# Normed queries and keys turned by VectorE's block transpose, through DRAM

## The chip, the cores and the metric

The kernel runs on one core of one Trainium2 chip. The core has TensorE (PE, matrix products), VectorE (DVE), ScalarE (ACT), GpSimd (POOL) and SyncE (SP, which here only issues transfers), and 16 DMA engines that move data between DRAM and the on-chip memory. The metric is the time of one execution on the device in microseconds, as the median of several runs.

## The reference, cut to what matters

`x` is 64 batches of 32 tokens with 512 channels, all in fp32. Four layers are added to it one after the other; the change concerns the third, attention with a paged cache of keys and values:

```python
q = rmsnorm(x @ Wq.T) * q_norm_w      # 32 heads of 128
k = rmsnorm(x @ Wk.T) * k_norm_w      # 8 heads of 128
v = x @ Wv.T
pos = cache_seqlens[:, None] + arange(32)
q, k = rope(q, pos), rope(k, pos)     # rotary: halves of 64 swapped and mixed
k_all = concat([k_cache[block_table], k])     # 16 pages of 32, then 32 new keys
v_all = concat([v_cache[block_table], v])
scores = (q @ k_all.T) / sqrt(128)    # 4 query heads share one key head
probs = softmax(where(valid, scores, -1e30))
x = x + (probs @ v_all) @ Wo.T
```

The other layers are a product with one of 16 small matrices per batch before it and after it, and a linear layer with low-rank additions.

## The kernel before, in words

**Tiling.** Four batches make a tile of 128 tokens, so there are 16 tiles. The eight key heads are cut into two groups of four. A *step* is one group and one tile (32 steps: all tiles of the first group, then all of the second); a *unit* is one batch of a step (128 units, of four key heads each). Two steps with neighbouring tiles make a *pair* (16 pairs).

**Order.** The whole order is written by hand. The program is a list of *slots*; `at(slot, place, what)` files a piece of work, and `slot(i)` emits the pieces of slot `i` in a fixed order of places on in-order engines. From slot 0 on, slot `i` computes the scores of one key head of one unit (two products, L839 and L842, 128 query rows by 544 keys), evacuates them with the mask (VectorE, L847), and takes the exponentials (ScalarE, L858). `flip` turns the shares of two slots ago on TensorE (L881, copied by VectorE at L883), and the values of three slots ago are multiplied (L891). Four slots are a unit, 16 a step, 32 a pair. In the same slots TensorE also projects the queries, keys and values of the next pair (L655): three blocks of seven products, one block for keys and values, two for two query heads each, put together by a two-level scheme that needs fewer products, whose sums VectorE makes (`take`, L667). Slots below 0 are the front: the first two layers for all tiles, turning the key pages of the first group, and the first pair's projections. After the last slot the output products (L1342) run alone.

**Norm and rotary before.** A tile of four heads (128 tokens, 4 x 128) goes through `Norm`: squares on ScalarE (L711), the power -1/2 on GpSimd (L716, L718), then on VectorE `scale` (L723), `straight` (L730), `swapped` (two halves, L742) and `sum` (L752). There are 160 such tiles: per pair two of keys and eight of queries. `norm_piece` is a small planner: called three times a slot, it takes the next piece if the slot's count of VectorE work (`busy`) allows. One slot after `sum`, `turn` makes four 128x128 transposes on TensorE (L757) into PSUM, and `keep` copies them with ScalarE (L769) into a tile that stays on chip: `qT_0`, `qT_1` for queries, `kT_new` for new keys. `begin` copies a batch's new keys into the 17th page of the unit's keys (L826).

**Transfers.** SyncE issues most transfers, in program order. `Unit` takes a keys' tile `kT` (two buffers) and issues 16 page loads of 64 KB, each with a page number read from a table (L787, L795). It does so four slots before the unit's first scores. Also on SyncE: `fetch_new` (a batch's new values, L817), the values' stores (L697), rotary tables (L595), the activations (L590), for the second group's pages a load and two transfers per page tile during the first group (L255, L288, L292), and the outputs of half the heads (L931). GpSimd issues the value gathers (L105) and the other outputs, and makes the masks (L810).

## Time and profile before

| | |
|---|---|
| three runs | 2455.72, 2458.07, 2463.95 us, median 2458.07 |
| profiled execution, first to last instruction (the one time recorded of it) | 2459.1 us, granted TensorE clock 0.999 |
| first scores (slot 0) | at 190 us |
| one pair of steps, middle of the run | 118 us |
| output products alone, about 2080 to the end | 379 us |
| DMA | 459 MB in 457888 packets, 187 GB/s on average |

The profile names an engine, a source line, the operation and the tiles it writes and reads (out<-in), with a count and durations. "SPq" rows are SyncE issuing transfers; the time is that of the issue, not of the transfer. A timeline row with xN merges N instructions, and its duration runs from the first one's start to the last one's end.

### The profile page before, as it was taken

The numbers are of one execution on the slowest core, as the hardware profiler recorded it, in microseconds if no ns is written. First come the engines' busy times: TensorE is split into PE (matmuls) and PEld (weight loads), VectorE is DVE, ScalarE is ACT, GpSimd is POOL, SyncE is SP. The second block draws the span as 40 slices with busy tenths as digits, with TensorE's granted clock in tenths as the row PEclk, the third lists the DMA queues.
The fourth block names the chain that finished last, engine by engine and source line by source line (L and its number), as shares of the span: only waits on it lengthen the run. The fifth ranks groups of instructions, "written<-read, shape, count | busy, mean of one in ns | idle before, by whom it ended". The sixth has DMA issues, their size and how long they took to land.

```text
span 2459.1 us, 47105 instructions
## 1 busy us (share of the span) xinstructions
PE 2414.3 (98%) x13760; PEld 1863.4 (76%) x13760; DVE 1671.4 (68%) x3604; ACT 1399.1 (57%) x4005; POOL 1188.6 (48%) x1163
## 2 busy tenths in 40 slices
PE   7998999999999999999999999999999999999999
PEld 4556777777777777777777777777777788888887
DVE  5766777777867777787777777777777766333222
ACT  2236767677777777677777777777676764000000
POOL 4435556555555556655556555556565663000000
PEclk9999999999999999999999999999999999999999
DMA  7876666666667677866666666566667874233221
GB/s 258 273 233 195 187 199 192 202 193 192 199 188 208 189 214 221 262 184 198 175 192 176 189 179 192 170 193 175 190 179 233 256 248 155 104 112 129 86 88 59
DMA packets 457888, 459.18 MB, mean 187 GB/s; under 512 B 52960, under 2 KB 381024, under 8 KB 453920
## 3 DMA queue, kind: packets, MB, share of 16 engines
q1 hardware_dynamic: 402560, 276.03, 37.0%
q0 software_dynamic: 55072, 180.14, 24.1%
q8 instruction: 111, 1.82, 0.3%
q14 instruction: 145, 1.19, 0.2%
HBM read 384.66 MB, written 79.69 MB: 189 GB/s over the span
## 4 chain that ended last, share of the span: by engine, by line
PE 90%; DMA 3%; issue 2%; DVE 2%; ACT 2%; SPq 1%; POOL 1%; DVEq 0%; ACTq 0%; POOLq 0%
PE proj_ps L655 22%; PE o_ps L891 17%; PE out_ps L1342 15%; PE s_ps L839 9%; PE pT_ps L881 8%; PE s_ps L842 8%; PE l_ps L494 3%; PE head_ps L757 3%; PE o_ps L904 1%; DMA kT<-kT 1%; DMA o<-oT 1%; SPq L795 1%; PE s_ps L874 1%; PE h_ps L478 1%; PE mix_ps L438 1%
## 5 line engine op out<-in xcount | busy, mean ns | idle before, releaser
L105 POOL DMA_INDIRECT v_sb<-v,v_rows x512 | 545.1, 1065 | 369.0 <-PE o_ps L891 255.0
L891 PE MATMUL o_ps<-pT,v_sb 128*128 128x128 f32 x4096 | 625.5, 275 | 7.9 <-DMA v_sb<-v,v_rows 3.2
L891 PEld LDWEIGHTS o_ps<-pT,v_sb 128*128 128x128 f32 x4096 | 576.8, 191 | 39.7 <-ACT oT L923 6.4
L858 ACT ACTIVATE sm<-sm,top 128x544 f32<-128x544 f32 x512 | 380.8, 744 | 320.7 <-DVE top L847 242.6
L847 DVE CUSTOM_DVE_ANT_0 sm<-s_ps,pen 128x544 f32<-128x544 f32 x512 | 369.0, 721 | 113.1 <-PE s_ps L842 98.8
L864 ACT ACTIVATE sm<-sm,share 128x512 f32<-128x512 f32 x512 | 369.9, 722 | 109.5 <-DVE share L863 73.9
L883 DVE COPY pT<-pT_ps 128x512 f32<-128x512 f32 x512 | 352.9, 689 | 69.3 <-PE pT_ps L881 22.9
L839 PE MATMUL s_ps<-kT,qT 128*128 128x288 f32 x1024 | 334.9, 409 | 2.4 <-DMA kT<-kT 1.3
L881 PE MATMUL pT_ps<-ident,sm 128*128 128x128 f32 x2048 | 309.7, 274 | 5.5 <-ACT qT L769 4.0
L842 PE MATMUL s_ps<-kT,qT 128*128 128x256 f32 x1024 | 304.9, 379 | 1.7 <-DMA kT<-kT 1.4
L667 DVE TENSOR_TENSOR raw<-proj_ps,raw 128x512 f32<-128x512 f32 x332 | 224.1, 687 | 114.5 <-PE proj_ps L655 103.2
L839 PEld LDWEIGHTS s_ps<-kT,qT 128*128 128x128 f32 x1024 | 179.2, 191 | 149.8 <-issue 129.1
L810 POOL TENSOR_SCALAR pen<-key_f,seq_f 128x544 f32<-128x544 f32 x128 | 283.7, 2216 | 12.8 <-DMA kT<-kT 1.5
L881 PEld LDWEIGHTS pT_ps<-ident,sm 128*128 128x128 f32 x2048 | 238.7, 141 | 9.6 <-ACT qT L769 5.2
L711 ACT ACTIVATE sq<-raw 128x128 f32<-128x128 f32 x640 | 198.5, 310 | 74.5 <-DVE raw L667 58.8
L842 PEld LDWEIGHTS s_ps<-kT,qT 128*128 128x128 f32 x1024 | 194.6, 190 | 56.4 <-issue 2.3
L863 DVE RECIPROCAL share<-total 128x1 f32<-128x1 f32 x512 | 83.6, 163 | 177.4 <-ACT sm L858 149.7
L716 POOL TENSOR_SCALAR ss<-ss 128x4 f32<-128x4 f32 x160 | 40.2, 251 | 326.3 <-ACT sq L711 320.0
L1392 ACT COPY p<-out_ps 128x256 f32<-128x256 f32 x7 | 2.6, 372 | 333.5 <-PE out_ps L1342 333.5
L655 PE MATMUL proj_ps<-sum,x 128*128 128x512 f32 x380 | 189.1, 600 | 0.0
L105 POOL DMA_INDIRECT mix_rows<-in_w,cond_rows x32 | 34.8, 1087 | 307.6 <-DVE mix_diag L170 299.5
L718 POOL TENSOR_TENSOR rstd<-ss,minus_half 128x4 f32<-128x4 f32 x160 | 167.8, 1049 | 13.3
(177 smaller groups left out, 3571.1 us busy)
## 6 DMA issues: line engine op xcount, KB each, us to landing
kT<-kT SPq DMA_DIRECT2D x2048, 64.0 KB
o_in<-o SPq DMA_DIRECT2D x28, 1024.0 KB
o<-oT POOLq DMA_DIRECT2D x69, 256.0 KB
o<-oT SPq DMA_DIRECT2D x58, 256.0 KB
page_rows<-in_kv_cache SPq DMA_DIRECT2D x32, 256.0 KB
v<-in_kv_cache SPq DMA_DIRECT2D x32, 256.0 KB
kT<-page_rows SPq DMA_DIRECT2D x32, 256.0 KB
vn<-raw SPq DMA_DIRECT2D x32, 256.0 KB
```

Of the source, the lines that this page charges most:

```text
L105: nc.gpsimd.indirect_dma_start(out=dst, out_offset=None, in_=table, in_offset=bass.IndirectOffsetOnAxis(ap=index, axis=0),)
L655: nc.tensor.matmul(self.ps, lhsT=self.pair.x[x][:, c if x == "b" else half.start + c, :], rhs=blocks(self.b)[w][:, c, :], start=(c == 0), ...
L810: nc.gpsimd.tensor_scalar(self.pen, key_f, seq_f[:, self.b : self.b + 1], BIG, ALU.is_ge, ALU.mult)
L839: nc.tensor.matmul(ps[:, first:HID], lhsT=q, rhs=self.kT[:, :n1, k, :], start=True, stop=True)
L842: nc.tensor.matmul(ps[:, HID : first + LA], lhsT=q, rhs=self.kT[:, n1:, k, :], start=True, stop=True)
L847: nc.vector.tensor_tensor_reduce(out=sm, in0=ps[:, first : first + LA], in1=self.pen, scale=1.0, scalar=3e38, op0=ALU.add, op1=ALU.min, ac ...
L858: nc.scalar.activation(sm, sm, AF.Exp, bias=top, scale=-1.0, accum_out=total)
L864: nc.scalar.activation(sm[:, :L], sm[:, :L], AF.Copy, scale=share)
L881: nc.tensor.transpose(ps[:, c, :], self.sm[k][:, c * P : (c + 1) * P], ident)
L883: nc.vector.tensor_copy(pT, ps)
L891: nc.tensor.matmul(o_of[self.s, k][:, self.j, :], lhsT=self.v[c][:, k * D : (k + 1) * D], rhs=self.pT[k][:, c, :], start=(self.j == 0 and ...
L1342: nc.tensor.matmul(ps[:, :HALF], lhsT=o[:, i, :], rhs=w[i // REP][:, i % REP, :], start=(i == 0), stop=(i == KG * REP - 1),)
```

## The change

The four-head tiles are normed in pairs, as tiles of 128 x (2 x 4 x 128): for queries, the two four-head tiles of one step that belong to one block; for keys, the tiles of the two steps of the pair. So there are 80 `Norm`s in place of 160, with 128x1024 operations. `sum` is moved from VectorE to GpSimd. `turn` becomes one VectorE transpose of 32x32 blocks: since a batch has 32 tokens, a block's rows are one batch, and the transposed block is 32 of the 128 head channels for that batch. `store` then writes it to a DRAM tile `qk`, four transfers for a tile of queries (one a batch) and eight for keys (one a batch and step), all on SyncE. The transfer puts the four blocks of 32 channels under one another. `fetch_heads` loads a batch's new keys and queries (128 x 640) behind the pages of its keys' tile, two slots before its first scores, and `scores` reads both from there. The tiles `kT_new`, `qT_0`, `qT_1`, the four TensorE transposes per tile, their evacuation and the copy in `begin` are gone. The planner gets costs per piece and takes any piece that is ready; projections start six slots ahead of a pair's window instead of one (`AHEAD`), and the front begins five slots earlier. The order between slots is otherwise as it was.

```diff
+    qk_dram = [
+        [dram.tile([NB, D, (1 + KG) * P], F32, name=f"qk_{g}_{t}") for t in range(NT)]
+        for g in range(NG)
+    ]
...
             def new(self):
-                return proj_pool.tile([P, REP, D], F32, name="raw", bufs=6)
+                return proj_pool.tile([P, 2, REP, D], F32, name="raw", bufs=4)
...
             def sum(self):
-                nc.vector.tensor_tensor(self.a, self.a, self.b, ALU.add)
+                a, b = [x.rearrange("p i h d -> p (i h d)") for x in (self.a, self.b)]
+                nc.gpsimd.tensor_tensor(a, a, b, ALU.add)
 
             def turn(self):
-                self.tp = ps_t.tile([P, REP, P], F32, name="head_ps", tag="t")
-                for h in range(REP):
-                    nc.tensor.transpose(self.tp[:, h, :], self.a[:, h, :], ident)
...
+                self.turned = self.raw.rearrange("p i h d -> p (i h d)").rearrange(
+                    "p (c m s) -> p c m s", c=NC, s=S
+                )
+                nc.vector.transpose(
+                    self.turned, self.a.rearrange("p i h (c e) -> p c (i h) e", c=NC)
+                )
+
+            def store(self):
+                pair = self.block.pair
+                for i in (0, 1) if self.i == KV else (self.i,):
+                    step = pair.steps[i]
+                    if self.i == KV:
+                        heads, first, n = slice(i * REP, (i + 1) * REP), 0, P
+                    else:
+                        heads, first, n = slice(0, 2 * REP), (1 + 2 * self.block.b) * P, 2 * P
+                    for j in range(NB):
+                        nc.sync.dma_start(
+                            out=qk_dram[step.g][step.t][j][:, first : first + n].rearrange(
+                                "(c e) f -> e c f", c=NC
+                            ),
+                            in_=self.turned[j * S : (j + 1) * S, :, heads, :].rearrange(
+                                "e c m s -> e c (m s)"
+                            ),
+                        )
...
-                self.kT = room["kT"].tile([P, NPP + 1, KG, PSIZE], F32, name="kT")
+                self.kT = room["kT"].tile([P, NPP + 1 + KG, KG, PSIZE], F32, name="kT")
...
+            def fetch_heads(self):
+
+                nc.sync.dma_start(
+                    out=self.kT[:, NPP:].rearrange("p n k s -> p (n k s)"),
+                    in_=qk_dram[self.g][self.t][self.j],
+                )
...
-                q = step_of[self.s].qT[k][:, self.j].rearrange("p h s -> p (h s)")
+                q = self.kT[:, NPP + 1 + k].rearrange("p h s -> p (h s)")
...
+        ROOM = 2.0
+        COST = {"scale": 1.2, "straight": 1.2, "swapped": 1.3, "turn": 1.2}
+        NEXT = {"scale": "straight", "straight": "swapped", "swapped": "turn"}
 
         def norm_piece(slot):
 
 
-            if not pieces or pieces[0][0] > slot or busy.get(slot, 0) >= 2 + (slot % 4 == 1):
+            for piece in pieces:
+                ready, norm, name = piece
+                if ready <= slot and busy.get(slot, 0) + COST[name] <= ROOM:
+                    break
+            else:
                 return
-            busy[slot] = busy.get(slot, 0) + 1
...
+            busy[slot] = busy.get(slot, 0) + COST[name]
+            getattr(norm, name)()
+            at_piece = pieces.index(piece)
+            if name == "turn":
+                pieces.pop(at_piece)
+                at(slot, "store", norm.store)
+                return
+            later = name == "swapped"
+            if later:
+                at(slot + 1, "take", norm.sum)
+            pieces[at_piece] = (slot + 2 * later, norm, NEXT[name])
...
-        AHEAD = 1
+        AHEAD = 6
...
         n = KG * len(units)
-        begin = -WINDOW - AHEAD - 10
-        ready = -6
+        front = -WINDOW - AHEAD
+        begin = front - 10
+        ready = front + 27
...
+            at(KG * u - 2, "fetch", call, unit_of, u, "fetch_heads")
             at(KG * u - 2, "act", call, unit_of, u, "begin")
```

## The prediction

> **What bounds the kernel now.** I read the page's first part, then the busy time by stage, then single queues. TensorE first:
>
> ```profile
> PE 2414.3 (98%) x13760; PEld 1863.4 (76%) x13760; DVE 1671.4 (68%) x3604; ACT 1399.1 (57%) x4005; POOL 1188.6 (48%) x1163
> ```
>
> A busy PE need not be PE at its peak, so the stages decide (PE, PEld, DVE, ACT, POOL busy; clock; DMA share; GB/s). The two long ones are one pair of steps each, 32 slots:
>
> ```profile
> 554.00:672.00 118.00, 117.73 (x717) 90.45 (x716) 89.20 (x199) 85.41 (x249) 66.56 (x64) 1.00 0.66 196
> 1498.00:1616.00 118.00, 117.76 (x715) 90.33 (x715) 89.59 (x200) 85.06 (x248) 66.87 (x64) 1.00 0.62 184
> 1970.00:2010.00 40.00, 38.25 (x273) 33.83 (x272) 23.33 (x55) 25.44 (x61) 26.11 (x27) 1.00 0.87 270
> ```
>
> In a pair TensorE idles 0.3 us of 118 at full clock: what is taken from it there is time, until another queue comes due. The transposes stand in the timeline of TensorE:
>
> ```profile
> 566.06 1.02 PE L655 MATMUL proj_ps<-sum,x 128*128 128x512 f32 x2
> 566.92 0.60 PE L757 MATMUL head_ps<-ident,rot_a 128*128 128x128 f32 x4
> 567.36 0.65 PE L839 MATMUL s_ps<-kT,qT 128*128 128x288 f32 x2
> ```
>
> Start to start, four cost 0.44 us, 0.11 each (the 273 ns of one is pipeline depth). They aren't hidden: the next scores start behind them.
>
> The engine that no busy share counts is SyncE, which only issues. Its timeline in the first group:
>
> ```profile
> 705.16 0.57 SPq L817 DMA_DIRECT2D v_new<-vn  x1
> 705.79 0.60 SPq L288 DMA_DIRECT2D v<-in_kv_cache  x1
> 706.49 0.55 SPq L292 DMA_DIRECT2D kT<-page_rows  x1
> 707.91 10.03 SPq L795 DMA_DIRECT2D kT<-kT  x16
> 717.99 0.61 SPq L817 DMA_DIRECT2D v_new<-vn  x1
> 722.71 9.41 SPq L795 DMA_DIRECT2D kT<-kT  x16
> 732.17 0.42 SPq L255 DMA_DIRECT2D page_rows<-in_kv_cache  x1
> 737.29 0.87 SPq L931 DMA_DIRECT2D o<-oT  x2
> 738.25 0.57 SPq L817 DMA_DIRECT2D v_new<-vn  x1
> 740.36 9.80 SPq L795 DMA_DIRECT2D kT<-kT  x16
> ```
>
> A unit's 16 key loads hold the queue 10.0 us out of 14.75 (four slots). Over 672 to 790 the eight loads' rows sum to 78.9 us, the other rows to 14.0, gaps of 0.06 between rows and some 0.8 of page-number reads before each unit add 8.3: 101.2 us of 118. In 1500 to 1617, where no pages are turned any more, the same count gives 97.0 of 117. SyncE is 83 to 86% full, and in order. Today that rarely shows:
>
> ```profile
> PE s_ps L842 <- DMA kT<-kT: 1.4, 2, 1.2
> PE s_ps L839 <- DMA kT<-kT: 1.3, 1, 1.3
> ```
>
> (waits of TensorE: total us, times, longest). In 1970 to 2010, where slots are short, TensorE already falls to 96% as key loads follow each other without a pause.
>
> **The change, part by part.**
>
> *Transposes.* 640 x 0.11 = -70 us of TensorE: 4.4 a pair, 66 in the fifteen full pairs, 4 in the front. Nothing replaces them on TensorE. A pair could fall from 118.1 to 113.7 in the first group and from 117.2 to 112.8 in the second: 14.2 and 14.1 a unit, 3.55 a slot.
>
> *ScalarE.* 160 evacuations (L769, 91.4 us) and 128 key copies (L826, 37.5 us) go: off the path, worth nothing in time.
>
> *VectorE.* Per tile, one scale 0.706, one straight 0.690, two halves of swapped 0.432 and one sum 0.749 make 3.0 us, 482 in all. Per double tile: a 128x1024 product took 1.21 (L619), so 1.21 + 1.21 + 2 x 0.69 = 3.8 us, 304 for 80, plus the block transposes, which the trace lacks. The nearest row is again the 128x1024 pass at 1.21: 97 us. The Trainium skill, "VectorE: DVE Perf Modes", section "The three transpose paths", speaks against that: 311 ns for one 128x128, which times eight is an estimated 2.5 us, 199 in all. By the row VectorE falls from 89.3 to 84.3 us a pair, by the rule it rises to 90.6; both stay under 113.7, so either gives zero. I take the row.
>
> *GpSimd.* The sum doubles L450's 128x512 (1.28 undisturbed): 2.5 us x 80 = 200, against 80 fewer power pairs (1.05 + 0.25): -104. GpSimd goes from 67 to 73 us a pair. But its two-input pass stops VectorE's: beside an L450 of 1.35 us (127.91 to 129.26) the L723 product that started at 128.05 took 1.76 instead of 0.67. By the planner's costs (ROOM, COST) two sums of the five in a pair stand in the same slot as the next tile's scale. Behind it on VectorE wait the takes and the next evacuation of scores, which TensorE needs one slot later. VectorE has 30 us of room a pair, so I take 0; the bound is rival two.
>
> *SyncE, the step that decides.* New per pair: 24 stores (8 for the keys, 4 for each of 4 query tiles) and 8 head loads. The stores lay 32 partitions into four row groups in DRAM, like L292 (0.55, the same kind of split); with the gap 0.61. Bounds: 0.39 (the plain o<-oT, 0.33) to 0.66 (L288, 0.60). A head load is a plain row load: 0.38 (L590), with gap and one more semaphore 0.45. Sum: 24 x 0.61 + 8 x 0.45 = 18.2 us, so 119.4 in the first group and 115.2 in the second: more than TensorE needs. The Trainium skill, "DMA: Bandwidth & Descriptors", section "Issuing engines are not separate DMA queues", calls the sequencer's time to initiate a DMA "usually small relative to the DMA itself". By that rule these steps cost nothing and the total would be about 2400; here the issue (0.35 for a key load) is longer than its 128 packets take on 16 engines (about 0.036 each by the queue's totals, 0.3), so I go by the row.
>
> Room is not shared freely: the keys' tile has two buffers, so a unit's loads can't start before the scores two units back end, and must land before its own begin, 16.65 us later (five slots less 1.1 of scores). Issue 10.05 and landing 1.3 (packet records) leave 5.3 us for lateness and everything between, as the head load stands behind. With the planner's slots (from a pair's first score):
>
> - Slots 0-3: last pair's 4 query stores, head load, rotary, values, o: the next window starts 4.8 late, and 4-7 leave 8-11 2.5 late.
> - Slots 8-11, the keys' eight stores: 2.5 + 10.05 + 4.9 + v_new 0.63 + 0.45 + 1.3 = 19.8, so TensorE waits 3.2.
> - Slots 20-23: 2.8 + 10.05 + 0.4 + 2.45 + 0.45 + 1.3 = 17.45: 0.8.
> - Slots 28-31: 3.4 + 10.05 + 0.43 + 2.45 + 0.63 + 0.45 + 1.3 = 18.7: 2.0.
> - The others fit. First group: 5.9 a pair. Second group, without page transfers (3.5 us): 3.1 + 1.0 = 4.1.
>
> The wait of the first store in a burst for VectorE's turn is met, as SyncE reaches it behind 10 us of loads. The head load in slot 30 needs stores issued in slot 28; the one it reads went first of four and has some 3 us to land: zero, at most 1.5 a pair. What is late next: a raw buffer is free only when its stores have landed; the copy in slot 5 needs the one stored at slot 0, with about 3 us left. Beyond that ScalarE, and the exponentials behind its copy, would stand.
>
> *DMA.* 42 MB written and 42 read again, at the hardware queue's 276 MB for 37%: 11% of the span, so about 0.66 becomes 0.8. Below the 0.87 of the tail: zero.
>
> *Order moved (AHEAD).* All of the front and every projection move five slots ahead. In the tail five slots lose their filler, where SyncE needs 13 us a unit anyway, and the last pair's stores and heads (2.45 + 8 x 0.45) join it: +7. At 180 to 210 TensorE now works 21 of 30 us before the first scores; the moved projections fill some of that, while sum, store, landing and head load (2.5 + 2 + 1.5, estimates from the rows above) lengthen the first tile's way: +4, so the front gives its 4 back.
>
> **Sum:** -70 + 8 x 5.9 + 7 x 4.1 + 7 + 4 = +17, on the profiled execution's span of 2459.1, which lies 1 above the runs' median of 2458.1: **2476**.
>
> **Rivals.**
>
> 1. *Not slower: issuing is cheaper.* At 0.50 a store the same windows give -18, at 0.40 about -46, thus 2412; 0.55 is the break-even. For it: plain rows cost 0.33 to 0.38, the query stores read one contiguous 4 KB row per partition. Against: every four-way DRAM split of SyncE in the trace cost 0.55 to 0.58 (L292, L817).
> 2. *VectorE becomes the bound.* If all five sums hold VectorE for 2.5 us where 1.5 of slack exists, 5 us a pair, 75 in all. Alone, with SyncE free, -70 + 11 + 75 = +16; on top of SyncE, half of it hidden behind its waits, 2510 to 2550. For: the 1.76. Against: by then the sum is mostly done when scale starts.
> 3. *It balances:* stores at 0.55, within 0.3% (7.4 us, about what a measurement can tell).
>
> That the change takes nothing off the path is excluded by the 0.3 us of idle.
>
> **How the numbers follow.** Forecast 0.50 (own range 2455 to 2515; 0.05 of it within 0.3%), cheaper issue 0.28 (2405 to 2450), VectorE or ScalarE on top 0.15 (2515 to 2570), balance 0.07. Faster 0.28, same 0.12, slower 0.60. Leaving out the outer part of both ends: 2415 to 2545.
>
> **What the next profile would show.** Right: no head_ps; DVE transposes near 1.2; TensorE waits for kT of several us a pair, once behind eight stores in slots 8-11; SyncE without pauses; store issues near 0.55. Wrong: TensorE still at 99% in a pair of about 114 (stores under 0.5), or waits on top or oT (VectorE, ScalarE) ahead of kT.

## The result, and the profile after

The changed kernel takes **2864.98 us** (median of four runs, 2861.84 to 2866.92) against 2456.89 us for the kernel before on the same chip (2453.82 to 2463.95). The ratio is **1.1654** (95% interval 1.1635 to 1.1673), so it is 17% slower. The prediction had the sign and missed the size: 2476, range 2415 to 2545. Its profiled execution spans 2865.1 us.

The first part of the page after, as shown of before:

```profile
PE 2487.0 (87%) x13120; PEld 1879.1 (66%) x13120; DVE 1648.9 (58%) x3204; ACT 1308.3 (46%) x3717; POOL 1347.9 (47%) x1083
```

No engine became the bound. TensorE issues 640 instructions fewer, yet its busy time rose by 73 us, and it now idles 378 us of the span (45 before). The busy time by stage says why both are so (one pair of steps of the first group, one of the second, and the stretch of the last group that was shown of before; columns as there):

```profile
491.00:637.00 146.00, 124.62 (x676) 92.36 (x676) 86.81 (x174) 79.76 (x229) 76.13 (x59) 0.92 0.66 194
1351.00:1493.00 142.00, 118.65 (x653) 88.69 (x652) 85.19 (x170) 76.91 (x222) 77.84 (x59) 0.92 0.63 187
1970.00:2010.00 40.00, 33.88 (x176) 25.28 (x175) 25.13 (x49) 21.82 (x66) 20.79 (x16) 0.96 0.54 153
```

A pair takes 142 to 146 us in place of 118. TensorE stands for 21 to 23 us of it, and the granted clock is 0.92 and no longer 1.00: what it does, it does more slowly. What TensorE waits for (total us, times, longest):

```profile
PE s_ps L905 <- DVE top L878: 93.2, 31, 6.2
PE s_ps L870 <- DMA kT<-qk: 71.0, 16, 13.3
PE s_ps L870 <- DMA kT<-kT: 62.5, 15, 11.5
PE s_ps L870 <- issue: 47.6, 13, 7.2
```

L870 is the first product of the scores, which needs a batch's pages and heads; L905 is the transpose of the shares of the new keys. The prediction knew of the first place only. SyncE's waits and ScalarE's, the same columns:

```profile
SPq L823 <- PE s_ps L873: 134.3, 39, 7.7
SPq L705 <- DVE raw L675: 105.7, 17, 11.7
...
SPq L793 <- DVE raw L780: 31.7, 22, 11.9
```

```profile
ACT oT L954 <- DMA o<-oT: 116.1, 23, 7.2
```

SyncE stands 106 us in front of the values' store (L705), until VectorE has made the last sum of that tile, and 32 us in front of stores of turned tiles (L793). ScalarE's wait for an output tile's buffer was 3.1 us in three times before; it is 116 now. The two places in the kernel before:

```profile
ACT oT L923 <- DMA o<-oT: 3.1, 3, 1.6
```

```profile
SPq L697 <- DVE raw L667: 2.1, 2, 1.8
```

**Where the 406 us between the two spans went.** TensorE's idle time between the first and the last scores rose from 19 to 338 us: +216 ahead of scores, +111 ahead of L905, -9 elsewhere. The first scores start at 211.8 us and not at 190.5: +21. The transposes give about 3.4 us a pair back (worked out below): -52 in fifteen and a half pairs. What follows the start of the last scores is the same (394.5 before, 394.0 after). The remainder, 406 - 318 - 21 + 52 = **119 us**, is what matrix products lost to the clock: 287 us of the attention ran at half clock, 3 before. A count that doesn't use the remainder agrees: TensorE is busy for 235 of these 287 us, and half of that is 117.

**The two waits in the timeline.** First a late head load, on TensorE and on SyncE:

```profile
1605.77 0.59 PE L663 MATMUL proj_ps<-wq,x 128*128 128x512 f32 x1
1611.40 0.99 PE L870 MATMUL s_ps<-kT 128*128 128x288 f32 x2 [5.04 <-DMA kT<-qk]
1612.18 1.06 PE L873 MATMUL s_ps<-kT 128*128 128x256 f32 x2
```

```profile
1603.92 2.04 SPq L793 DMA_DIRECT2D qk<-raw  x4
1606.00 0.64 SPq L854 DMA_DIRECT2D kT<-qk  x1
```

The head load stands behind 16 key loads and four stores, is issued at 1606.00, and TensorE can go on 5.4 us later. The products behind the gap take 0.99 and 1.06 us for two; with the full clock they take 0.65 and 0.59. Then a late output buffer, on ScalarE, GpSimd and TensorE:

```profile
1515.47 1.07 ACT L954 COPY oT<-o_ps 128x512 f32<-128x512 f32 x2 [0.67 <-PE proj_ps L663]
...
1519.94 0.56 ACT L954 COPY oT<-o_ps 128x512 f32<-128x512 f32 x1
1526.83 0.59 ACT L954 COPY oT<-o_ps 128x512 f32<-128x512 f32 x1 [6.32 <-DMA o<-oT]
```

```profile
1521.54 0.60 POOL L962 DMA_DIRECT2D o<-oT  x1
```

```profile
1530.17 0.47 PE L905 MATMUL s_ps<-ident,p_new 128*128 128x128 f32 x1 [5.38 <-DVE top L878]
```

A step has four outputs, copied by ScalarE into `oT`, which has three buffers. The fourth copy starts 0.1 us after the store that GpSimd issued at 1521.54 for the *third* has landed (the semaphore comes at 1526.73, 5.2 us after the issue). The next exponentials stand behind that copy on ScalarE, the evacuation of the next scores behind them, and TensorE waits 5.4 us. Before, the fourth copy followed the third within 0.5 us in 27 of 31 steps (564.35 and 564.82, for one, merged in this row of before):

```profile
564.35 1.05 ACT L923 COPY oT<-o_ps 128x512 f32<-128x512 f32 x2
```

The instruction lists as built show the difference (HW are transfers that SyncE issues, SW those of GpSimd; the fourth copy of one step, before and after):

```
L923 TensorCopy oT_7171<-o_ps_6451 128x512 [waits DMAHW6_49,PE_49]
L954 TensorCopy oT_6823<-o_ps_6163 128x512 [waits DMASW5_49,PE_49,Activation_49]
```

Before, it takes the buffer of the step's first output, which SyncE stored some 3 us earlier; after, in 19 of 32 steps, that of the output just copied, which GpSimd stores. The trace agrees: in 19 steps the fourth copy waits for the semaphore of that store of GpSimd's, and 113 of ScalarE's 116 us of waits are for such stores. Of the 112 us of idle time ahead of L905, 88 lie in the 19 gaps around a late fourth copy. Nothing in the diff says so: which buffer a tile gets is settled when the program is built. That SyncE's longer list shifted it is an inference; e22 below, which only adds stores to the kernel before, shifts it too.

### The profile page after: what moved, and what is told of

Same layout as the page of the kernel before. It is cut to its first block, busy times and chain, and to the rows that moved or that the text cites. A ratio compares the mean times of both kernels' runs of the same rounds, so it can differ in the third digit from the quotient of the medians.

```text
span 2865.1 us, 45876 instructions
## 1 busy us (share of the span) xinstructions
PE 2487.0 (87%) x13120; PEld 1879.1 (66%) x13120; DVE 1648.9 (58%) x3204; ACT 1308.3 (46%) x3717; POOL 1347.9 (47%) x1083
## 4 chain that ended last, share of the span: by engine, by line
PE 50%; SPq 13%; issue 11%; DMA 10%; ACT 8%; DVE 6%; POOL 1%; ACTq 0%; POOLq 0%; DVEq 0%
PE out_ps L1381 13%; PE proj_ps L663 11%; SPq L823 7%; PE o_ps L922 7%; PE s_ps L870 6%; PE s_ps L873 4%; ACT sq L722 4%; ACT sm L889 3%; PE pT_ps L912 3%; DMA o<-oT 3%; PE l_ps L502 2%; SPq L793 2%; DMA kT<-qk 2%; DMA kT<-kT 2%; DVE raw L675 2%
## 5 line engine op out<-in xcount | busy, mean ns | idle before, releaser
L105 POOL DMA_INDIRECT v_sb<-v,v_rows x512 | 583.2, 1139 | 571.3 <-PE o_ps L922 462.5
L922 PE MATMUL o_ps<-pT,v_sb 128*128 128x128 f32 x4096 | 655.5, 285 | 4.2 <-ACT oT L954 4.2
L922 PEld LDWEIGHTS o_ps<-pT,v_sb 128*128 128x128 f32 x4096 | 610.0, 201 | 42.3 <-ACT oT L954 9.7
L870 PE MATMUL s_ps<-kT 128*128 128x288 f32 x1024 | 368.1, 443 | 232.6 <-DMA kT<-qk 71.0
L870 PEld LDWEIGHTS s_ps<-kT 128*128 128x128 f32 x1024 | 193.3, 200 | 497.0 <-issue 401.3
L873 PE MATMUL s_ps<-kT 128*128 128x256 f32 x1024 | 325.9, 402 | 0.0
L912 PEld LDWEIGHTS pT_ps<-ident,sm 128*128 128x128 f32 x2048 | 256.9, 148 | 0.5
L873 PEld LDWEIGHTS s_ps<-kT 128*128 128x128 f32 x1024 | 208.4, 203 | 62.1
L773 POOL TENSOR_TENSOR rot_a<-rot_a,rot_b 128x1024 f32<-128x1024 f32 x80 | 189.5, 2368 | 88.1 <-DVE rot_b L764 86.1
L1381 PE MATMUL out_ps<-w,o_in 128*128 128x256 f32 x768 | 167.1, 379 | 0.1
L1381 PEld LDWEIGHTS out_ps<-w,o_in 128*128 128x128 f32 x768 | 145.8, 190 | 20.2 <-POOL same L130 0.5
```

What stands on the lines that cost most here:

```text
L105: nc.gpsimd.indirect_dma_start(out=dst, out_offset=None, in_=table, in_offset=bass.IndirectOffsetOnAxis(ap=index, axis=0),)
L870: nc.tensor.matmul(ps[:, first:HID], lhsT=q, rhs=self.kT[:, :n1, k, :], start=True, stop=True)
L873: nc.tensor.matmul(ps[:, HID : first + LA], lhsT=q, rhs=self.kT[:, n1 : NPP + 1, k, :], start=True, stop=True)
L912: nc.tensor.transpose(ps[:, c, :], self.sm[k][:, c * P : (c + 1) * P], ident)
L922: nc.tensor.matmul(o_of[self.s, k][:, self.j, :], lhsT=self.v[c][:, k * D : (k + 1) * D], rhs=self.pT[k][:, c, :], start=(self.j == 0 and ...
L1381: nc.tensor.matmul(ps[:, :HALF], lhsT=o[:, i, :], rhs=w[i // REP][:, i % REP, :], start=(i == 0), stop=(i == KG * REP - 1),)
```

## The experiments

All are edits of the changed kernel, save the last. Ratios are to the kernel before on the same chip (2446 to 2458 us), so gains are taken between ratios; 0.01 is 24.5 us. Idle time and half clock are those between the first and the last scores of the profiled run; "steps" are those whose fourth output copy waits for the store of the third that GpSimd issued.

| run | ratio (95%) | idle ahead of scores | ahead of the new keys' transpose | at half clock | steps |
|---|---|---|---|---|---|
| before | 1 | 3 | 1 | 3 | 0 |
| after | 1.1654 (1.1635 to 1.1673) | 219 | 112 | 287 | 19 |
| e1 values' store later | 1.1344 (1.1290 to 1.1398) | 230 | 43 | 201 | 6 |
| e2 heads early | 1.1400 (1.1373 to 1.1427) | 162 | 133 | 275 | 20 |
| e3 six stores a pair, heads gathered | 1.2681 (1.2655 to 1.2706) | 420 | 91 | 514 | 13 |
| e4 e1+e2+e3 | 1.1816 (1.1797 to 1.1836) | 342 | 25 | 324 | 0 |
| e5 sum on VectorE | 1.1708 (1.1682 to 1.1733) | 209 | 119 | 276 | 20 |
| e6 six stores a pair, plain rows | 1.1343 (1.1291 to 1.1395) | 168 | 102 | 222 | 13 |
| e7 e1+e2 | 1.0947 (1.0919 to 1.0975) | 163 | 51 | 187 | 7 |
| e8 e1+e2+e6 | 1.0777 (1.0750 to 1.0804) | 160 | 27 | 147 | 0 |
| e11 three keys' tiles | 1.1352 (1.1316 to 1.1388) | 168 | 119 | 230 | 19 |
| e12 AHEAD = 8 | 1.1719 (1.1673 to 1.1764) | 285 | 30 | 330 | 7 |
| e13 e8, AHEAD = 8 | 1.0842 (1.0812 to 1.0872) | 134 | 47 | 147 | 0 |
| e14 e13, more buffers | 1.0788 (1.0762 to 1.0814) | 156 | 21 | 141 | 0 |
| e15 fixed heads | 1.1663 (1.1637 to 1.1690) | 222 | 111 | 299 | 19 |
| e16 fixed heads, no stores | 1.0781 (1.0759 to 1.0803) | 91 | 91 | 137 | 13 |
| e17 e8, ScalarE issues | 1.1584 (1.1560 to 1.1609) | 137 | 174 | 256 | 29 |
| e18 e17, GpSimd stores | 1.1365 (1.1340 to 1.1390) | 98 | 186 | 224 | 29 |
| e21 e16+e1+e2 | 1.0175 (1.0158 to 1.0192) | 50 | 25 | 26 | 0 |
| e22 before + 24 stores | 1.0471 (1.0452 to 1.0490) | 15 | 3 (72 elsewhere) | 82 | 14 |

**e1: the values' store behind the key loads.** With AHEAD = 6 this store fell into slot 3, in front of the outputs and of slot 4's key loads; before, it lay in slot 8, behind key loads.

```diff
-                        at(last, "store", block.store_values, i // 5)
+                        at(last + 1, "store", block.store_values, i // 5)
```

> The store of a tile's new values is filed one slot later, so that SyncE reaches it behind the 16 key loads of that slot and not ahead of them; nothing else changes, and the number of transfers is the same. Order theory (SyncE stands in front of this store until VectorE's last take, and the outputs, whose copies ScalarE needs before its exponentials, come late behind it): TensorE's waits at L905 for the row maximum, 112 us, fall below 20, the time at half clock falls from 303 to about 200 us, total about 2700. Count theory (only how many transfers SyncE has to issue matters): nothing changes, 2850 to 2880. Landing theory (the head load lands too late): waits at L905 stay or move to L870, 2820 to 2880.

2775.61 us; 76 us less by the ratios. The waits ahead of L905 fall from 112 to 43 (the order theory had them below 20) and half clock by 87, as it said; the gain is half of what it gave, since the waits ahead of scores don't move (219 and 230). SyncE's wait at L705 is gone, so it was not what made the scores wait. Two causes are not told apart here: SyncE comes to its output stores earlier, and in the program as built the fourth copy now has GpSimd's buffer in 6 steps and not 19. ScalarE's waits for an output buffer:

```profile
ACT oT L954 <- DMA o<-oT: 37.9, 16, 6.5
```

**e2: heads ahead of the pages.**

```diff
                 self.kT = room["kT"].tile(...)
+                if u > 1 and u % (2 * NB):
+                    self.fetch_heads()
...
-            at(KG * u - 2, "fetch", call, unit_of, u, "fetch_heads")
+            if u < 2 or u % (2 * NB) == 0:
+                at(KG * u - 2, "fetch", call, unit_of, u, "fetch_heads")
```

> The load of a batch's heads goes ahead of the 16 page loads of its own tile, two slots earlier, except where its stores are not yet out (the first two units of the run and the first of each pair). The number of transfers is the same. Landing theory (a head load needs 3.5 us or more to land, behind 16 key loads that end just before the scores): TensorE's waits at L870, about 200 us, fall below 80, half clock falls to about 200 us, total 2640 to 2720. Count theory: no change, 2850 to 2880. Order theory: L870 waits stay near 200, at most 30 us gained.

2789.24 us, 62 us less. Waits ahead of scores fall by 57, those for the heads to 11 us in two times: late landing is real, but smaller than its theory had it (waits ahead of scores below 80, 2640 to 2720 us). In the changed kernel the last packet of a head load (320 KB) comes 3.5 us after the start of its issue on the median and 5.4 in the slowest twentieth. The prediction had taken 1.3, the packet records of a 64 KB key load.

**e3: one store for a double tile and step, six a pair, and the head load gathers.**

```diff
-        [dram.tile([NB, D, (1 + KG) * P], F32, name=f"qk_{g}_{t}") for t in range(NT)]
+        [dram.tile([NB, S, NC, (1 + KG) * P], F32, name=f"qk_{g}_{t}") for t in range(NT)]
...
-                    for j in range(NB):
-                        nc.sync.dma_start(
-                            out=qk_dram[step.g][step.t][j][:, first : first + n].rearrange(
-                                "(c e) f -> e c f", c=NC
-                            ), ...
+                    nc.sync.dma_start(
+                        out=qk_dram[step.g][step.t].rearrange("j e c f -> (j e) c f")[
+                            :, :, first : first + n
+                        ], ...
...
-                    in_=qk_dram[self.g][self.t][self.j],
+                    in_=qk_dram[self.g][self.t][self.j].rearrange("e c f -> c e f"),
```

> The DRAM tile is laid out so that one transfer stores a whole double tile (six stores for a pair of steps in place of 24); the bytes stay the same, the head load gathers its four row groups instead of one plain row. Count theory (the prediction's: 24 stores of 0.6 us fill SyncE): 18 issues of 0.45 to 0.6 us less for each of 15 pairs, 120 to 160 us, and with the stalls half of the lost clock, total 2640 to 2720. Order and landing theories: the waits at L905 (112 us) and L870 (200 us) shrink by less than a third, total 2780 to 2850.

3102.62 us, 251 us *more* by the ratios. No theory had that. The stores are not the reason: the gathered head load now lands after 7.4 us (10.0 in the slowest twentieth), with 3.4 of its packets in flight at a time where the plain load has 7.7. The Trainium skill, "DMA: Bandwidth & Descriptors", section "Rules for kernel authors", says that the slowest dimension of the access patterns sets how many DMA engines a transfer uses, so that an outermost size of 4 confines it to 4 engines. The measured 3.4 agrees with that; the same bytes land 3.9 us later.

**e4: e1, e2 and e3 together.**

> All three together: values' store a slot later, heads ahead of the pages, one store for a double tile. If order, landing and count are all that the change costs, TensorE's idle time in the attention falls from 332 to below 50 us and its clock returns above 0.99, so the total comes to about 2400 to 2430, below the kernel before (2457), since 640 transposes (70 us) are gone. If VectorE's turn, the raw tiles or GpSimd's sum hold the queue as well, 100 us or more of idle stays: 2520 to 2650.

2891.64 us: the slow head load, in front of the key loads, made SyncE wait 327 us in 122 times. As a test of the sum it says nothing; e8 repeats it.

**e6: six stores, plain rows.** The channels are kept interleaved, in the key pages too, so that the head load is 128 plain rows.

```diff
-                nc.sync.dma_start(
-                    out=kT_dram[self.g][4 * c : 4 * c + 4].rearrange("p d f -> d p f"), ...
+                to = kT_dram[self.g][4 * c : 4 * c + 4].rearrange("p (e c) f -> c e p f", c=NC)
+                for i in range(NC):
+                    nc.sync.dma_start(out=to[i], in_=self.turned[i * S : (i + 1) * S]. ...)
...
-                    in_=qk_dram[self.g][self.t][self.j],
+                    in_=qk_dram[self.g][self.t][self.j].rearrange("e c f -> (e c) f"),
```

> Six stores for a pair of steps in place of 24 again, but with the channels in another order (four row groups interleaved, the key pages stored in the same order), so that a batch's heads are 128 plain rows for the head load as in the changed kernel. The store of a turned page tile costs four transfers in place of one for this. Spread theory (the run with one store and a gathered head load lost 238 us because that load is moved by some four DMA engines at a time and lands after 7.4 us in place of 3.5): the head load's last packet is back near 3.5 us and the time is at most 2865. Count theory: 18 issues of about 0.48 us less for a pair, 3 us more for the pages in the first group, with the stalls 80 to 120 us, total 2740 to 2790. Order and landing theories: 2820 to 2870. If one large store is itself the cause of the loss, 3000 or more.

2779.25 us, 76 less than after and 328 less than e3: the number of stores counts, and e3's loss was its head load's shape. The head load lands after 3.5 us again.

**e7 and e8: the edits together.**

> The values' store a slot later and the heads ahead of the pages, with the 24 stores as in the changed kernel. If order and landing are two separate causes their gains add: 2865 - 90 - 76 = 2700, waits at L905 (L907 here) below 50 us and waits for the heads below 20. If one only moves the wait to the other, 2750 to 2790.

2682.17 us: 173 us less, more than the 138 of the two alone. Neither moves the wait to the other.

> All three: values' store a slot later, heads ahead of the pages, six stores in place of 24 with plain rows for the head load. If the three causes are separate: the sum of the gains of the single runs, about 2600 to 2650. If SyncE's count is what remains once order and landing are mended, the gain of the six stores is now larger than alone: 2450 to 2600. If VectorE's turn or GpSimd's sum is what SyncE waits for, no more than 30 us below the run with two.

2642.15 us, 42 below e7. The three gains taken alone add up to 214 us, and together they give 215: this fits separate causes, though on top of the other two the six stores bring 42 and not 76. No fourth copy waits for GpSimd any more, and away from the start of a pair most units take 13 to 16.5 us. More than half of what is left sits ahead of the first scores of each pair, 9.1 us on the mean of five pairs in the middle of the run and 7.1 over the last fifteen:

```profile
705.29 10.54 SPq L824 DMA_DIRECT2D kT<-kT  x16
715.93 0.60 SPq L794 DMA_DIRECT2D qk<-raw  x1
...
717.26 0.93 SPq L707 DMA_DIRECT2D vn<-raw  x1
719.47 0.81 SPq L855 DMA_DIRECT2D kT<-qk  x2
```

```profile
725.08 1.30 PE L871 MATMUL s_ps<-kT 128*128 128x288 f32 x2 [9.36 <-DMA kT<-kT]
```

The keys' buffer was free at 699.7; SyncE came to these loads at 705.3, since rotary tables, activations and a page tile stood in between, and to the first heads of the pair, which this run leaves behind the pages, at 719.5.

**e11: three buffers for the keys' tile.**

```diff
-                    room["kT"] = l2.enter_context(tc.tile_pool(name="kT", bufs=2))
+                    room["kT"] = l2.enter_context(tc.tile_pool(name="kT", bufs=3))
```

> The changed kernel with three buffers for the keys' tile in place of two, nothing else. Window theory (the prediction's: a unit's loads can't start before the scores two units back end, so lateness of SyncE becomes a stall): SyncE's waits at L823 for L873, 134 us, vanish, TensorE's waits at L870 shrink by half, total 2690 to 2760. In-order theory (SyncE is held by its own waits for VectorE, in program order, and can't run ahead whatever buffers are free): 2820 to 2870.

2781.36 us, 74 less: between the two theories. The window of two tiles is real (SyncE's 134 us of waits for a free tile are gone, the waits ahead of scores fall from 219 to 168), and the waits ahead of L905 stay.

**e12, e13, e14: more lead for the projections.**

```diff
-        AHEAD = 6
+        AHEAD = 8
```

> The changed kernel with AHEAD = 8 in place of 6, nothing else: all projections, turns and stores stand two slots (7 us) earlier against the scores. Chain theory (a pair's last turn, its stores, their landing and the head load behind them fill more time than the two slots between them, so the first unit of a pair waits): the wait ahead of a pair's first scores, 4.1 us on the mean, falls below 1, about 15 times 4 us and half as much for the clock, total 2770 to 2800. Order, landing and count theories: the other waits only move, 2830 to 2880.

2867.56 us, nothing gained: the waits ahead of L905 fall to 30 us, those ahead of scores rise to 285.

> The run with all three (values' store later, heads ahead of the pages, six stores) and AHEAD = 8. In that run TensorE waited 9.1 us ahead of the first scores of each pair and under 1 us elsewhere, and the unit after such a wait ran partly at half clock. Chain theory: both go, 15 times 9 us and about 7 us of clock for each wait, 2640 - 240 = 2400 to 2450, no longer slower than the kernel before. If the wait is the head load's own time and not the lateness of the turn, it stays: 2600 to 2650.

2651.07 us. The wait ahead of a pair is 6.3 us in place of 9.1 (5.7 in place of 7.1 over the last fifteen), others appear: the chain theory falls.

```diff
-                oT = room["attn"].tile([P, REP, P], F32, name="oT", bufs=3)
+                oT = room["attn"].tile([P, REP, P], F32, name="oT", bufs=4)
```

> As the run before this one, with the first heads of a pair ahead of the pages too, three buffers for the keys' tile and four for the copied outputs (SyncE waited 110 us for that copy in the run with all three). If a window of two tiles still costs something: 10 to 40 us less than with AHEAD = 8 alone, 2380 to 2430. If nothing but TensorE bounds by then: the same within 10 us.

2639.25 us. ScalarE no longer waits for an output buffer at all, but by then little hung on it. The first head load of a pair, now ahead of the pages, makes SyncE wait for the landing of the store it reads (72 us in 15 times), and the key loads behind it are late. What these edits gain together over e13 is 13 us, and the two intervals just overlap.

**e5: the sum on VectorE.**

```diff
-                nc.gpsimd.tensor_tensor(a, a, b, ALU.add)
+                nc.vector.tensor_tensor(a, a, b, ALU.add)
```

> The changed kernel with the sum of the rotary on VectorE (128x1024, 1.2 us) in place of GpSimd (2.4 us), nothing else. Contention theory (rival 2: GpSimd's sum stops VectorE's products, whose lateness reaches the scores): the scale falls from 1.59 to about 1.2 us, TensorE's waits for the row maximum fall by half, total 2780 to 2820. If the sum only lies elsewhere: 2850 to 2890, VectorE's busy time up by 97 less 30 us.

2864.83 us, no gain. The scale falls from 1.59 to 1.21 us, as foreseen, and no wait changes much: GpSimd's sum does slow VectorE, and nothing waits for that.

**e15 and e16: heads without dependence, then no stores.**

```diff
-                    in_=qk_dram[self.g][self.t][self.j],
+                    in_=qk_dram[0][self.t % 2][self.j],
```

> The changed kernel, in which every head load reads the DRAM tiles of the first pair of steps (the scores of all later pairs are those of other tokens, that part of the computation is left out); stores, loads, bytes and order are the same, but no head load depends on a recent store. Chain theory (turn, store, landing and head load follow each other too closely): the first unit of a pair no longer waits (4.1 us on the mean), total 2770 to 2810. Order, landing and count theories: 2840 to 2870.

2866.23 us, no difference: in the changed kernel the way from a store to the load that reads it costs nothing.

```diff
                 pair = self.block.pair
+                if pair.steps[0] is not pair_of[0].steps[0]:
+                    return
```

> As the run before this one, and the stores of the normed queries and keys are left out behind the first pair (the turns on VectorE stay). SyncE issues 24 transfers less for a pair, about 11.5 us, and no longer waits for turns (32 us). Count theory: 110 to 200 us below the run before this one. If SyncE's issues had room: no more than the 32 us of waits and their clock, 50 us.

2649.42 us, 217 below e15: the stores are the largest single item. TensorE's waits, to be read beside those of after:

```profile
PE s_ps L907 <- DVE top L880: 90.8, 34, 6.2
PE s_ps L872 <- DMA kT<-qk: 27.6, 9, 13.9
PE s_ps L872 <- DMA kT<-kT: 20.3, 4, 7.1
```

All kinds together, the waits ahead of scores fall from 222 us in e15 to 91, half clock from 299 to 137. The waits ahead of L905 gain less (111 to 91, with 13 steps), so most of what the stores cost here is late keys and heads. The edit takes out three things at once: the issues, SyncE's waits for turned tiles, and 42 MB of writes. The writes don't show in the packets, as one of 512 bytes in SyncE's queue takes 27.9 ns on the mean before, 28.1 after and 27.9 here; the other two are not told apart.

**e17 and e18: other queues issue.** ScalarE issues the page stores of the second group and half the outputs; in e18 GpSimd also issues the stores of turned tiles.

```diff
-        queue = nc.sync if k < 2 and s < len(steps) - 3 else nc.gpsimd
+        queue = nc.scalar if k < 2 and s < len(steps) - 3 else nc.gpsimd
```

> The run with all three (2642 us), with the stores of turned pages, the copies of the cached values and half of the outputs issued by ScalarE in place of SyncE: 5 to 7 us of issues a pair and SyncE's wait for the copied outputs (110 us) go from SyncE; ScalarE is half idle and made most of this data itself. If SyncE, full to the brim ahead of slot 28, is what makes the first unit of a pair wait 9.1 us: that wait falls below 4 us, total 2520 to 2580. If the wait has another cause: 2620 to 2660.

> As the run before this one, and the six stores of a pair are issued by GpSimd, which has made the sums that are turned. SyncE then waits for no turn. If SyncE's waits in program order are the rest of the loss: 20 to 80 us below the run before this one, 2450 to 2550. If the way turn, store, landing, load is itself too long for the slots it has: no more than 15 us between the two; if GpSimd's own queue of gathers comes late behind its waits, slower.

2844.98 and 2796.13 us: 198 and 144 us *slower* than e8. SyncE was relieved (waits ahead of scores 137 and 98), but with the outputs on another queue the fourth copy takes GpSimd's buffer in 29 steps, ScalarE waits 167 and 165 us for an output buffer, and ScalarE's own issues (64 us in e17) stand in front of exponentials. What these runs were to tell, whether a full SyncE explains e8's rest, they tell only in part.

**e21: everything found, taken out.** e16, e1, and e2 for every unit but the first two.

> The run without stores (behind the first pair; head loads read the first pair's tiles, so the later scores are those of other tokens), with the values' store a slot later and the heads ahead of the pages for every unit but the first two. It asks whether stores, order and landing are the whole loss. If their gains simply add: 2649 - 90 - 76 = 2483, or 2466 with the 183 of both together. If they are the whole loss and TensorE bounds again, its idle time in the attention below 40 us and its clock above 0.99: 2385 to 2425. If VectorE's turns or GpSimd's sums hold something too: 2500 to 2650.

2501.05 us, still 43 above the kernel before (ratio 1.0175), of them 18 in the front. A pair takes 118.6 us with 4.1 idle in the first group and 117.5 with 4.1 in the second, at full clock: work of 114.5 and 113.4, against 118.0 - 0.2 and 117.2 - 0.2 before. So the transposes were worth 3.3 to 3.6 us a pair. With stores, order and landing out of the way the attention is nearly back, and even then the change has no gain left. The theory that they are the whole loss had TensorE idle for less than 40 us in the attention; it idles 82, and what holds it is not shown.

**e22: 24 stores added to the kernel before,** from a constant tile, in the same slots.

```diff
+        for i in range(n_pairs):
+            home = WINDOW * (i - 1)
+            for w, b, which in ((8, KV, 0), (17, 0, 0), (21, 0, 1), (28, 1, 0), (32, 1, 1)):
+                at(home + w, "store", more_store, i, b, which)
```

> The kernel before, with its transposes on TensorE, to which SyncE's 24 stores for a pair of steps are added in the slots and the shapes of the changed kernel, from a constant tile, so that nothing waits for them and they wait for nothing; their data is not used. The prediction's arithmetic of windows, without head loads and with slots of 14.75 us: some 2 us of stall a pair, 2470 to 2500. If the 24 issues themselves cost what leaving them out of the changed kernel gave (217 us): 2620 to 2680. If they only cost with their waits and with the head loads behind them: 2450 to 2465.

2573.65 us, 115 more; none of the three theories. TensorE's waits and ScalarE's:

```profile
PE pT_ps L887 <- ACT qT L775: 38.8, 10, 5.8
PE pT_ps L887 <- ACT p_new L871: 18.6, 5, 5.2
PE s_ps L845 <- DMA kT<-kT: 7.1, 4, 3.2
```

```profile
ACT oT L929 <- DMA o<-oT: 69.4, 19, 6.6
```

The keys' windows, on which the prediction's whole sum rested, cost 15 us in the run, half of what that arithmetic gave (2 us a pair). The loss is the output buffer: 14 steps, about one a pair, in 13 of which ScalarE waits 4 to 6.6 us, TensorE behind it, and 82 us of half clock. So a part of what stores on SyncE cost in these kernels is the buffer that the program as built gives the fourth copy.

## Why the prediction was wrong

By its own steps. The sum came to +17 and the two spans differ by 406, so 389 us are to be found: 140 in the stalls ahead of scores (216 and not 76), 119 in the clock and 111 in the waits ahead of L905, both put at nothing, 18 in the transposes and 17 in the front; less 9 of idle time elsewhere and the 7 of the tail, which the measured terms hold already.

**Transposes, -70.** Measured 3.3 to 3.6 us a pair, some -52: 0.083 to 0.09 for one and not 0.11. So four in a row, taken start to start, overstated what their removal gives.

**VectorE and GpSimd, zero.** Right. The block transpose takes 1.226 us (98.1 in 80), so the row chosen was the right one of the two and the 2.5 us worked out from the skill's page was not (the page's 311 ns is for a bf16 tile, and this one is fp32). GpSimd's sum takes 2.37 us and slows the scale to 1.59; e5 shows that this costs nothing. Rival 2 falls. The two rows (count | busy us, mean ns | idle us ahead):

```profile
L780 DVE STREAM_TRANSPOSE raw<-rot_a 128x1024 f32<-128x1024 f32 x80 | 98.1, 1226 | 0.0
L738 DVE TENSOR_TENSOR raw<-raw,rstd 128x1024 f32<-128x1024 f32 x80 | 127.0, 1587 | 0.0
```

**SyncE, "the step that decides".** The queue was the right one, and e16 shows the stores to be the largest item. The stalls were mis-sized: ahead of scores, put at 5.9 and 4.1 us a pair (the three of the first group add up to 6.0), they are about 14 (219 us in 15.5 pairs). The price of one issue was not what was too small: a store issue takes 0.44 us on the median and 0.50 with its gap, not 0.61, and with 0.50 rival 1 had the kernel faster (-18). Two terms of the window arithmetic were at fault: "landing 1.3" was used for the heads, and it is 3.5 to 5.4 (e2: 62 us); and "the wait of the first store in a burst is met" was wrong (32 us in 22 waits), presumably since SyncE, once late, is no longer always late at the same place. The values' store, named only as one issue, is a wait of 106 us; e1 shows that it costs at the outputs and not ahead of the scores. How the rest of the 219 us follows from the windows is not shown. In the kernel before, which has longer slots and loads no heads, 24 such stores a pair cost the key windows only 15 us (e22).

**"What is late next".** This is the step that failed outright. The prediction asked which buffer is freed late and named the raw tiles, for which VectorE waits 10.5 us at most in any run; its last section then listed a wait on `oT` only as a sign of being wrong. The one that shows is `oT`, three buffers for four outputs, whose copy stands in front of the exponentials: 112 us of idle time ahead of L905, 88 of them around a late fourth copy. In the changed kernel these are the steps with GpSimd's buffer, and with fewer of them the waits ahead of L905 are shorter (19, 13, 7, 6, 0 steps in after, e16, e7, e1, e8: 112, 91, 51, 43, 27 us). But that buffer is not the only way to a late copy: in e4, e12 and e13, with 0, 7 and 0 such steps, ScalarE waits 62, 85 and 52 us for output stores that SyncE issued. In a single step the timeline shows the cause; a run with four output buffers and nothing else changed wasn't made, and why the builder picks that buffer is only argued.

**Clock: no term.** The sum assumed the full clock. Behind the gaps of 5.04 and 5.38 us shown above the clock is 0.5 for 3.4 us, and there are 59 such stretches in the run, of 3.4 us or a multiple of it. Of TensorE's gaps in the attention, counted by length, half clock sets in during the gap or within 3.5 us behind it for none of the 39 of 0.5 to 2 us, 6 of the 10 of 2 to 3 us, 14 of the 17 of 3 to 4 us, and all 36 longer ones. The Trainium skill, "TensorE: Matmul & The Clock Gate", section "Why this matters for your kernels", asks for no idle gaps above about 3 us between bursts of matmuls, as one idle window brings the half rate back. The traces agree, only that gaps of 2 to 3 us were often enough here. The rule should have stood beside each stall of the prediction: its own 3.2 us at slots 8 to 11 was long enough (before has one gap of 3.2 us, at 206 us, and half clock for 3.4 us behind it). For the fifteen stalls of 3.1 or 3.2 us that it had this would have been some 26 us, by estimate (15 times half of 3.4). Most of the 119 us, of 406, came with the stalls that it didn't have.

**Order moved.** The tail fits in number: the last pair, which has no projections beside it, takes 110.1 us from its first scores to its last and not 103.3, +6.8 for +7. But TensorE idles only 2.6 us more there, and the rest goes with a clock of 0.95, so this is luck in part. The front was put at no loss (4 us longer, 4 given back), and the first scores come 21 us later. 12 of these 21 us are a longer wait of TensorE right before them (13.3 us for the first head load, 1.3 at that place before). But with AHEAD = 8 (e12) this wait is 1.2 us and the first scores still come 17 us later, so why the front is longer stays open.

**Head load in slot 30, "zero, at most 1.5 a pair"** was right in the changed kernel (e15: no difference). "DMA 11% more: zero" had no run of its own; the packets of 512 bytes named at e16 took no longer (27.9 ns before, 28.1 after).

**What stays open.** e8 still waits 7 to 9 us a pair; its timeline shows SyncE late, but moving issues to other queues disturbed the output buffers at the same time, so no run isolates it. No version here beats the kernel before.

## What to carry to other kernels

When work is added to an in-order queue, list everything whose *release* hangs on that queue, not only what it loads: a buffer with one copy too few, freed by a store, can stop an engine that has nothing to do with the change, and which buffer that is may shift with the build (0 steps of 32 before, 19 after). Price a transfer's landing by its own size and place in the queue, not by a smaller neighbour's. And where a stall passes 2 to 3 us, add the half clock behind it.

## What the runs showed of the hardware that was not expected

- Stalls cost about a third more than their length here: 318 us of added idle time brought 119 us of loss at half clock. With the idle time nearly gone (e21) 26 us of half clock are left in the attention, of 287.
- The same 320 KB land after 3.5 us as 128 plain rows of DRAM and after 7.4 as four groups of 32 (e6 and e3, which differ otherwise in the page stores alone, and by 328 us of run time).
- A 256 KB store issued by GpSimd landed 5.2 us after its issue (1521.54 to 1526.73).
